# Softmax reciprocals turned through DRAM in a decoder layer's attention

## The chip, the cores and the metric

The kernel runs on one core of a Trainium2 chip. The core has five engines with a queue of instructions each: TensorE (PE in the profile, with its weight loads as PEld), VectorE (DVE), ScalarE (ACT), GpSimd (POOL) and SyncE (SP), which here only issues transfers. Engines wait for each other through semaphores. Transfers are issued by SP, ACT or POOL and are carried out by 16 DMA engines that all the issuers share. The metric is the device time of one execution in microseconds (us); lower is better.

## The reference

One decoder layer on x of 8 x 256 x 512, all in float32: self-attention with 16 heads of width 32, then an elementwise recurrence with the context (its decay is per head), then a feed-forward part (FFN) whose weights are splines of given control points. After each comes a residual and a layer norm. What matters here is the attention:

```python
q_r = jnp.einsum('bhtd,dr->bhtr', q, Wdown)
k_r = jnp.einsum('bhtd,dr->bhtr', k, Wdown)
v_r = jnp.einsum('bhtd,dr->bhtr', v, Wdown)
scores = jnp.einsum('bhqr,bhkr->bhqk', q_r, k_r) * scale
attn = jax.nn.softmax(scores, axis=-1)
y_r = jnp.einsum('bhqk,bhkr->bhqr', attn, v_r)
y = jnp.einsum('bhtr,rd->bhtd', y_r, Wup)
y = y.transpose(0, 2, 1, 3).reshape(B, T, D)
out = y @ Wo.T
```

The down and up projections are folded into the weights of q, k, v and of the output.

## The kernel before

The 2048 tokens (8 sequences of T = 256) are worked through in NG = 4 groups of 512 tokens, two sequences each. The projections of a group (`project`, 48 units of one matmul call in 12 chains) and the output projections of a finished sequence (`output`, units of the kind "o") are kept in the list `units`; `fill(n)` (321) takes n of them, and so puts them between the parts of the attention. The order of work is written by hand: the wrapper `Ordered` (266) keeps every engine's instructions in program order, so each engine's queue runs in the order in which the code below emits it.

The attention runs in 32 steps, `for s, (g, bb, quad) in enumerate(steps)` (701). A step is one quad of four heads of one sequence, n = 2g + bb; each sequence has quads 0 to 3. The steps are pipelined by one: in step s the scores (`scores`, 468) of step s + 1 are started, the exps of step s + 1 are emitted head by head with `ahead(0)` to `ahead(3)` (729), and the exps that step s - 1 has left in `es` are transposed (`transposed`, 502), copied out of PSUM (`evicted`, 509) by DVE, ACT, DVE and ACT in turn, and multiplied with v (`weighted`, 514).

- `exponentials` (486): DVE takes the negated maximum over the keys, `nmax`, with queries on the 128 partitions; ACT makes `e = exp(sc + nmax)` for each half of the queries and accumulates the sums, so that `sums[n]` is [128 queries, 2 halves, 16 heads].
- The four heads' score tiles `sc` lie in the four PSUM buffers of `ps_big`. The scores of the next step can only be written when the exps have read them.
- `weighted` writes `av`, a PSUM tile [128, 2, 256] whose partitions are (head of the quad, r) and whose free axis is the query; two quads share one `av`. It is not yet divided by the softmax sums.
- The division needs the reciprocal of the sums in the layout of `av`: the head on partitions, each value over 32 partitions, the query along the free axis. The sums lie the other way round. In odd quads (733 to 737) DVE takes the reciprocals `rec` of the eight heads of two quads and copies them 32 times, into `wide`. Late in the same step (756 to 767), behind `fill(6)`, PE turns `wide` round in four transposes into the PSUM tile `tr_rec`, and ACT copies that to `y` (tile yT in the profile).
- The pair `y, av` is left in `pending` (772). The next step multiplies it on DVE, `y = av * y` (745), behind the first eviction of that step; `output` then reads `y`. The last pair is multiplied behind the loop (775), just ahead of the FFN.

The pool `ps_mm` has four PSUM buffers, which transposes, projections, outputs, `tr_rec` and `av` share. In groups 0 to 2 `fill` finds the projections of the next group; in group 3 there are none, and each step takes `fill(2)` twice: outputs, and the first `inputs` (642) of the FFN, which turn x2 round, write it to DRAM and load it back in another order (`xd`, `md`, `xg`). Taps for the FFN weights are loaded by SP and combined by POOL all through the attention (`taps`, 387). ACT issues no transfers before the change but the seven at the very start (582 to 585).

The lines that decide where things stand in a step:

```python
        eTs.append(evicted(tr1, nc.scalar.copy))
        ahead(1)
        eTs.append(evicted(tr2, nc.vector.tensor_copy))
        fill(2)
        tr3 = transposed(es[3])
        ahead(2)
        eTs.append(evicted(tr3, nc.scalar.copy))
        ahead(3)
        fill(6 if g + 1 < NG else 2)
```

Of the kernel before, what the change touches and what calls it, by code (L numbers as in the profile page):

```python
# [10 lines left out]
F32 = mybir.dt.float32  # L11
# [6 lines left out]
P = 128  # L18
B, T, D = 8, 256, 512
NH, DH = 16, 32  # L20
# [262 lines left out]
def decoder_kernel(ctx: ExitStack, tc: tile.TileContext, x, xT, ctxT, wq, wkT, wvT, woT, wdownT, wup, decay, up_taps, down_taps, mom_f, sum_f, out, plan):  # L283
    nc = tc.nc
# [4 lines left out]
    small = ctx.enter_context(tc.tile_pool(name="small", bufs=4, side="left"))  # L289
    rows = ctx.enter_context(tc.tile_pool(name="rows", bufs=6, side="left"))  # L290
    ps_big = ctx.enter_context(tc.tile_pool(name="ps_big", bufs=4, space=PSUM))
    ps_mm = ctx.enter_context(tc.tile_pool(name="ps_mm", bufs=4, space=PSUM))
    ident = const.tile([P, P], F32, name="ident")
# [11 lines left out]
    done = ExitStack()  # L305
    last = done.enter_context(tc.tile_pool(name="last", bufs=1, side="right"))
    mid = ExitStack()
    att = mid.enter_context(tc.tile_pool(name="att", bufs=1, side="right"))
# [3 lines left out]
    nc = Ordered(tc)  # L312
# [8 lines left out]
    def fill(n):  # L321

        for i in range(n):
            if units:
                next(units[0][1])
                units[0][2] -= 1
                if not units[0][2]:
                    units.pop(0)
            if i % 2:
                slot()  # L330
                some_taps()
# [53 lines left out]
    folded, qkvs, rs, sums, xs, yTs = {}, {}, {}, {}, {}, {}  # L385
# [34 lines left out]
    def load_x(g):  # L420
        xT_g = early.tile([P, DC, GT], F32, tag="xT", name="xT_g")
        nc.sync.dma_start(out=xT_g, in_=xT[:, g * GT : (g + 1) * GT].rearrange("(c p) t -> p c t", p=P))
        return xT_g
# [24 lines left out]
    def projections(g, xT_g):  # L448
        qkvs[g] = group_tiles(g)
        return [[name, project(g, name, m, xT_g), DC] for name in "qkv" for m in range(DC)]  # L450

    def recur(n):

        r = last.tile([P, DC, T], F32, tag="r", name="r", bufs=2)
        nc.sync.dma_start(out=r, in_=ctxT[:, n * T : (n + 1) * T].rearrange("(c p) t -> p c t", p=P))
        rs[n] = r
        yield
        yield
        nc.gpsimd.tensor_tensor(r, r, r, ALU.mult)
        yield  # L460
        yield
        for ch in range(DC):
            nc.vector.tensor_tensor_scan(
                r[:, ch, :], dec[:, ch : ch + 1].to_broadcast([P, T]), r[:, ch, :], 0.0, ALU.mult, ALU.add
            )
            yield

    def scores(s):

        g, bb, quad = steps[s]  # L470
        qT, kT, _ = qkvs[g]
        t0 = bb * T
        sc = [ps_big.tile([P, 2, T], F32, tag="big", name="sc") for _ in range(4)]
        for qc in range(2):
            for j in range(4):
                at = slice(j * DH, (j + 1) * DH)
                nc.tensor.matmul(
                    sc[j][:, qc, :],
                    lhsT=qT[at, quad, t0 + qc * P : t0 + (qc + 1) * P],
                    rhs=kT[at, quad, t0 : t0 + T],  # L480
                    start=True,
                    stop=True,
                )
        return sc
# [17 lines left out]
    def transposed(e):  # L502
        tr = ps_mm.tile([P, 2, T], F32, tag="mm", name="tr_e")
        for kc in range(2):
            for qc in range(2):
                nc.tensor.transpose(tr[:, kc, qc * P : (qc + 1) * P], e[:, qc, kc * P : (kc + 1) * P], ident)
        return tr

    def evicted(tr, copy):
        eT = att.tile([P, 2, T], F32, tag="eT", name="eT", bufs=4)  # L510
        copy(eT, tr)
        return eT
# [16 lines left out]
    def load_rows(n):  # L529
        xs[n] = []  # L530
        for qc in range(2):
            x_t = rows.tile([P, D], F32, tag="row", name="x_t")
            r0 = (n * 2 + qc) * P
            nc.sync.dma_start(out=x_t, in_=x[r0 : r0 + P, :])
            xs[n].append(x_t)

    def output(n, qc):

        ps = ps_mm.tile([P, D], F32, tag="mm", name="ps_o")
        for c in range(DC):  # L540
            nc.tensor.matmul(
                ps,
                lhsT=yTs[n][c // 2][:, c % 2, qc * P : (qc + 1) * P],
                rhs=w_o[:, c, :],
                start=(c == 0),
                stop=(c == DC - 1),
            )
            if c < DC - 1:
                yield
        h1 = rows.tile([P, D], F32, tag="row", name="h1")  # L550
        s1 = small.tile([P, 1], F32, tag="s1", name="s1")
        nc.vector.scalar_tensor_tensor(h1, ps, 1.0, xs[n][qc], ALU.mult, ALU.add, accum_out=s1)
        chains.append(norms(n, qc, h1, s1))
        yield
# [78 lines left out]
    def open_inputs():  # L633
        pool = ctx.enter_context(tc.tile_pool(name="inputs", bufs=1, side="left"))
        ffn["pool"] = pool
        ffn["dram"] = ctx.enter_context(tc.tile_pool(name="dram", bufs=2, space=bass.MemoryType.DRAM))
        ffn["mf"] = pool.tile([P, DC, 2, K2], F32, name="mf")
        nc.sync.dma_start(out=ffn["mf"], in_=mom_f)
# [58 lines left out]

    pending = None  # L700
    for s, (g, bb, quad) in enumerate(steps):
        n = g * 2 + bb
        if quad == 0 and bb == 0:
            if g + 1 < NG:
                units += projections(g + 1, xT_g)
            else:
                first.close()
                open_inputs()
                units += [["i", inputs(0), 2 * DC], ["i", inputs(1), 2 * DC]]
        if quad == 0 and n:  # L710
            load_rows(n - 1)
            o = [["o", output(n - 1, qc), DC] for qc in range(2)]
            if bb and g + 1 < NG:
                units[1:1] = o[:1]
                units.append(o[1])
            else:
                units[1:1] = o
            chains.append(recur(n))
        more = s + 1 < len(steps)
        if more and steps[s + 1][0] != g:  # L720
            while any(u[0] != "o" for u in units):
                fill(4)
            if g + 2 < NG:
                xT_g = load_x(g + 2)
        if more:
            sc = scores(s + 1)
        after = []

        def ahead(j):
            if more:  # L730
                after.append(exponentials(s + 1, j, sc[j]))

        if quad % 2:
            rec = small.tile([P, 2, 8], F32, tag="rec", name="rec")
            nc.vector.reciprocal(rec, sums[n][:, :, quad // 2 * 8 : quad // 2 * 8 + 8])
            wide = att.tile([P, 2, 8, DH], F32, tag="wide", name="wide")
            nc.vector.tensor_copy(wide, rec.unsqueeze(3).to_broadcast([P, 2, 8, DH]))
        tr0 = transposed(es[0])
        ahead(0)
        eTs = [evicted(tr0, nc.vector.tensor_copy)]  # L740
        tr1 = transposed(es[1])
        tr2 = transposed(es[2])
        if pending is not None:
            y, av = pending
            nc.vector.tensor_tensor(y, av, y, ALU.mult)
            pending = None
# [4 lines that stand above are left out]
        tr3 = transposed(es[3])  # L751
        ahead(2)
        eTs.append(evicted(tr3, nc.scalar.copy))
        ahead(3)
        fill(6 if g + 1 < NG else 2)
        if quad % 2:
            tr = ps_mm.tile([P, 2, T], F32, tag="mm", name="tr_rec")
            for q in range(2):
                for qc in range(2):
                    nc.tensor.transpose(  # L760
                        tr[:, q, qc * P : (qc + 1) * P],
                        wide[:, qc, q * 4 : q * 4 + 4, :].rearrange("p h r -> p (h r)"),
                        ident,
                    )
            y = last.tile([P, 2, T], F32, tag="yT", name="yT", bufs=4)
            nc.scalar.copy(y, tr)
            yTs.setdefault(n, []).append(y)
        else:
            av = ps_mm.tile([P, 2, T], F32, tag="mm", name="av")
        weighted(s, eTs, av)  # L770
        if quad % 2:
            pending = y, av
        es = after
    y, av = pending
    nc.vector.tensor_tensor(y, av, y, ALU.mult)
# [204 lines left out]
```

## Time and profile before

| | |
|---|---|
| median of 3 runs | 632.89 us (632.06 to 634.3) |
| the profiled execution | 633.12 us |
| its span in the profile | 631.3 us, 9965 instructions |
| granted clock of TensorE | 0.996 |
| busy: PE, DVE, ACT, POOL | 604.9, 334.5, 277.6, 210.1 us |
| SP's queue (q1) | 35656 packets, 63.24 MB, 32.9% of 16 engines |
| ACT's queue (q10) | 1008 packets, 1.18 MB, 0.6% |
| POOL's queue (q0) | 2048 packets, 6.77 MB, 3.5% |
| packets under 512 B, all queues | 4776 |

In the profile every operation of the kernel carries the line of the wrapper, L275, so groups are told apart by the names of their tiles, written out<-in. A row of the timeline has the start in us from the span's start, the duration, the engine, the operation, how many were merged, and in brackets the idle time ahead of it with what ended it. A matmul call on float32 shows as two MATMUL records, a transpose as one; matmuls are pipelined, so four records of 274 ns each that follow each other take less than four times that. The engine name with a q (SPq, ACTq) is a sequencer issuing a transfer.

### The profile page before, as it was taken

Reading aid. Unit: us, or ns where it says so; the run is one execution under the profiler, and the core shown is the slowest. Engines: PE = TensorE matmul, PEld = TensorE weight load, DVE = VectorE, ACT = ScalarE, POOL = GpSimd, SP = SyncE. Lnnn points to the kernel's source line nnn. Section 1 sums busy time; section 2 is a strip of 40 time slices with the busy share of each in tenths; the row PEclk is TensorE's granted clock in tenths of the full one; section 3 lists DMA queues with packets and bytes.
Section 4 is the critical chain, followed back from the end, with each engine's and each line's share of the span. In section 5 each row is a group of like instructions: output and inputs, shape, how many; then the busy total and the mean of one; then the engine's idle time right before and its main releaser. Section 6 shows DMA issues by size and latency. Waiting matters only on the chain.

```text
span 631.3 us, 9965 instructions
## 1 busy us (share of the span) xinstructions
PE 604.9 (96%) x3436; PEld 306.5 (49%) x3436; DVE 334.5 (53%) x741; ACT 277.6 (44%) x820; POOL 210.1 (33%) x479
## 2 busy tenths in 40 slices
PE   6999999998999999999999999999999999999993
PEld 2544555554555545555545564444443444444542
DVE  0203545666884756974847787767073235307304
ACT  0114635547474556563556675652061134206202
POOL 0001986265624343733403122014303601520242
PEclk9999999999999999999999999999999999999998
DMA  8104252044214134314104646652047717744501
GB/s 303 39 0 149 82 183 85 20 134 151 54 47 152 51 96 138 84 47 137 34 2 151 152 106 172 182 175 68 2 141 221 204 40 228 195 125 142 176 18 67
DMA packets 38763, 71.83 MB, mean 114 GB/s; under 512 B 4776, under 2 KB 9128, under 8 KB 38584
## 3 DMA queue, kind: packets, MB, share of 16 engines
q1 hardware_dynamic: 35656, 63.24, 32.9%
q0 software_dynamic: 2048, 6.77, 3.5%
q10 hardware_dynamic: 1008, 1.18, 0.6%
q8 instruction: 27, 0.44, 0.3%
q14 instruction: 24, 0.20, 0.1%
HBM read 43.39 MB, written 11.01 MB: 86 GB/s over the span
## 4 chain that ended last, share of the span: by engine, by line
PE 85%; DVE 9%; ACT 3%; issue 1%; DMA 1%; POOL 0%; POOLq 0%; DVEq 0%; ACTq 0%
PE y L275 12%; PE ps_k L275 9%; PE ps_v L275 9%; PE ps_s L275 9%; PE ps_o L275 8%; PE ps_q L275 7%; PE tr_e L275 6%; PE sc L275 5%; PE pg L275 4%; PE av L275 4%; PE pu L275 4%; DVE nmax L275 3%; PE ps_mom L275 2%; ACT e L275 2%; DVE eT L275 2%
## 5 line engine op out<-in xcount | busy, mean ns | idle before, releaser
L275 ACT ACTIVATE e<-sc,nmax 128x256 f32<-128x256 f32 x256 | 120.0, 479 | 101.3 <-DVE nmax L275 101.2
L275 DVE TENSOR_REDUCE nmax<-sc 128x2 f32<-128x512 f32 x128 | 84.4, 681 | 73.0 <-PE sc L275 67.0
L275 POOL TENSOR_TENSOR taps<-taps 128x256 f32<-128x256 f32 (+1 forms) x144 | 89.1, 619 | 33.9 <-DMA taps<-in_down_taps 24.7
L275 PEld LDWEIGHTS tr_e<-ident,e 128*128 128x128 f32 x512 | 56.9, 140 | 25.3 <-issue 22.5
L275 PE MATMUL tr_e<-ident,e 128*128 128x128 f32 x512 | 68.3, 276 | 0.6 <-DVE eT L275 0.5
L275 PE MATMUL ps_k<-xT_g,w_k 128*128 128x512 f32 x128 | 61.6, 625 | 6.2 <-DMA xT_g<-in_xT 5.6
L275 PE MATMUL y<-inter,wd 32*128 32x512 f32 x512 | 64.0, 610 | 0.0
L275 PE MATMUL ps_o<-w_o,yT 128*128 128x512 f32 x128 | 60.0, 600 | 2.0 <-DVE eT L275 1.7
L275 PE MATMUL ps_v<-w_v,xT_g 128*128 128x512 f32 x128 | 58.6, 598 | 0.0
L275 PE MATMUL ps_q<-xT_g,w_q 128*128 128x512 f32 x128 | 58.2, 596 | 0.0
L275 PE MATMUL ps_s<-nat,sf 128*128 128x512 f32 x128 | 56.0, 595 | 0.0
L275 POOL TENSOR_SCALAR va<-ss 128x1 f32<-128x1 f32 x32 | 7.1, 220 | 144.3 <-ACT x L275 83.4
L275 ACT ACTIVATION_READ_ACCUMULATOR e<-sc,nmax 128x1 f32 x256 | 53.1, 208 | 0.0
L275 POOL TENSOR_TENSOR rs<-va,neghalf 128x1 f32<-128x1 f32 x48 | 28.1, 585 | 70.7 <-DVE va L275 68.0
L275 DVE TENSOR_TENSOR inter<-pu,sg 128x512 f32<-128x512 f32 x64 | 41.2, 686 | 14.8 <-ACT sg L275 11.3
L275 ACT ACTIVATE sg<-pg 128x512 f32<-128x512 f32 x64 | 37.4, 597 | 15.3 <-PE pg L275 15.0
L275 DVE COPY eT<-tr_e 128x512 f32<-128x512 f32 x64 | 43.7, 683 | 0.5 <-PE tr_e L275 0.4
L275 PE MATMUL av<-eT,v_g 128*32 128x256 f32 x512 | 36.7, 385 | 5.0 <-ACT eT L275 2.7
L275 PEld LDWEIGHTS ps_k<-xT_g,w_k 128*128 128x128 f32 x128 | 24.0, 199 | 32.1 <-issue 24.1
L275 PEld LDWEIGHTS y<-inter,wd 32*128 32x128 f32 x512 | 25.6, 184 | 28.7 <-issue 26.5
L275 PEld LDWEIGHTS ps_s<-nat,sf 128*128 128x128 f32 x128 | 24.0, 190 | 31.7 <-issue 29.2
L275 ACT COPY eT<-tr_e 128x512 f32<-128x512 f32 x64 | 37.4, 585 | 2.4 <-PE tr_e L275 2.4
(94 smaller groups left out, 741.6 us busy)
## 6 DMA issues: line engine op xcount, KB each, us to landing
nat<-inter SPq DMA_DIRECT2D x128, 128.0 KB
taps<-in_down_taps SPq DMA_DIRECT2D x40, 256.0 KB
taps<-in_up_taps SPq DMA_DIRECT2D x16, 384.0 KB
r<-in_ctxT SPq DMA_DIRECT2D x8, 512.0 KB
x_t<-in_x SPq DMA_DIRECT2D x16, 256.0 KB
out<-o SPq DMA_DIRECT2D x16, 256.0 KB
xT_g<-in_xT SPq DMA_DIRECT2D x3, 1024.0 KB
xg<-xd SPq DMA_DIRECT2D x4, 704.0 KB
```

The costliest lines, as they stand in the source:

```text
L275: return lambda *a, **k: self.tc.keep_in_program_order(f(*a, **k))
```

## The change

The copy to `wide`, the four transposes and ACT's copy to `y` go. In their place the reciprocals are written with the heads ahead of the halves, stored to a DRAM tile `rd` of [16, 128] by a transfer that ACT issues at the head of the step (each partition holds 16 values, and each goes to another row of `rd`, 512 bytes apart), and read back by two transfers, also issued by ACT, behind its second eviction. Each read takes the four heads of one quad, 1 KB of 256 queries each, and repeats each row over 32 partitions (`[0, DH]`). The reads wait for the store. `y` is taken from its pool at that place, and so ahead of `ahead(3)` and `fill`. `rd` has two buffers.

```diff
+    turned = done.enter_context(tc.tile_pool(name="turned", bufs=2, space=bass.MemoryType.DRAM))
     pending = None
     for s, (g, bb, quad) in enumerate(steps):
...
         if quad % 2:
-            rec = small.tile([P, 2, 8], F32, tag="rec", name="rec")
-            nc.vector.reciprocal(rec, sums[n][:, :, quad // 2 * 8 : quad // 2 * 8 + 8])
-            wide = att.tile([P, 2, 8, DH], F32, tag="wide", name="wide")
-            nc.vector.tensor_copy(wide, rec.unsqueeze(3).to_broadcast([P, 2, 8, DH]))
+
+            rec = small.tile([P, 8, 2], F32, tag="rec", name="rec")
+            at = slice(quad // 2 * 8, quad // 2 * 8 + 8)
+            nc.vector.reciprocal(rec, sums[n][:, :, at].rearrange("p q h -> p h q"))
+            rd = turned.tile([8 * 2, P], F32, tag="rd", name="rd")
+            nc.scalar.dma_start(out=rd.rearrange("k p -> p k"), in_=rec.rearrange("p h q -> p (h q)"))
         tr0 = transposed(es[0])
         ahead(0)
...
         tr3 = transposed(es[3])
         ahead(2)
         eTs.append(evicted(tr3, nc.scalar.copy))
+        if quad % 2:
+            y = last.tile([P, 2, T], F32, tag="yT", name="yT", bufs=4)
+            for q in range(2):
+                from_ = bass.AP(rd.tensor, rd.offset + q * 4 * T, [[T, 4], [0, DH], [1, T]])
+                nc.scalar.dma_start(out=y[:, q, :], in_=from_)
+            yTs.setdefault(n, []).append(y)
         ahead(3)
         fill(6 if g + 1 < NG else 2)
-        if quad % 2:
-            tr = ps_mm.tile([P, 2, T], F32, tag="mm", name="tr_rec")
-            for q in range(2):
-                for qc in range(2):
-                    nc.tensor.transpose(
-                        tr[:, q, qc * P : (qc + 1) * P],
-                        wide[:, qc, q * 4 : q * 4 + 4, :].rearrange("p h r -> p (h r)"),
-                        ident,
-                    )
-            y = last.tile([P, 2, T], F32, tag="yT", name="yT", bufs=4)
-            nc.scalar.copy(y, tr)
-            yTs.setdefault(n, []).append(y)
-        else:
+        if quad % 2 == 0:
             av = ps_mm.tile([P, 2, T], F32, tag="mm", name="av")
         weighted(s, eTs, av)
         if quad % 2:
-            pending = y, av
+            pending = yTs[n][-1], av
```

## The prediction

> **What bounds it now.** First the page's chain of work that ended last, by engine; then the windows view, cut where the attention's fill work runs out (335) and where it ends (404). The columns are the stretch, its sum, busy time and count of PE, PEld, DVE, ACT and POOL, the clock, the DMA share and GB/s.
>
> ```profile
> PE 85%; DVE 9%; ACT 3%; issue 1%; DMA 1%; POOL 0%; POOLq 0%; DVEq 0%; ACTq 0%
> ```
>
> ```profile
> 60.00:139.00 79.00, 78.78 (x461) 42.28 (x458) 43.38 (x83) 42.59 (x145) 52.22 (x96) 1.00 0.36 112
> 150.00:335.00 185.00, 182.70 (x1078) 98.31 (x1077) 124.04 (x282) 102.23 (x341) 77.76 (x142) 1.00 0.27 81
> 335.00:404.00 69.00, 62.78 (x474) 35.68 (x472) 54.08 (x128) 45.06 (x151) 15.13 (x23) 1.00 0.55 147
> ```
>
> Up to 335 TensorE is the path (busy 78.78 of 79.00, 182.70 of 185.00): each step (score, exp, transpose, weigh: about 11 us) is filled with projections of the next group, and DVE and ACT wait. The last group, 335 to 404, has little to fill with: PE drops to 62.78 of 69.00, DVE rises to 54.08, and transfers keep the DMA engines 0.55 busy. The chain in order of time for this stretch runs through DVE:
>
> ```profile
> 353.00 0.59 DVE eT L275
> 353.60 0.60 DVE yT L275
> 354.20 0.60 DVE nmax L275
> 354.80 0.60 DVE eT L275
> ```
>
> The second of these pieces is the multiply of av by y that the change will feed from a DMA.
>
> **What goes.** The change touches the 16 odd steps of 32 (quad 1 and 3), numbered 0 to 31 here. The groups view (busy, mean ns of one, idle before):
>
> ```profile
> L275 PE MATMUL tr_rec<-ident,wide 128*128 128x128 f32 x64 | 9.7, 274 | 0.8 <-DVE mom L275 0.8
> L275 ACT COPY yT<-tr_rec 128x512 f32<-128x512 f32 x16 | 9.4, 588 | 12.0 <-PE tr_rec L275 12.0
> L275 DVE COPY wide<-rec 128x512 f32<-128x512 f32 x16 | 9.3, 584 | 0.5
> ```
>
> PE: four transposes a step; from the first tr_rec to the first av is 0.53 us in the timeline (81.09 to 81.62), and PE's queue closes up by that. The ACT copy (0.59) and the DVE copy (0.43 at its median) lie in those engines' waits, except step 17, where a wide of 1.68 us stands on the chain at 251.98; its nmax then waits for PE's scores (begun at 251.79, 0.5 to the first pair), so about 1.2 us come back. Ten odd steps are clear of what follows (1 to 21 without 7): 10 x 0.53 + 1.2 = **6.5 us gained**. The permuted reciprocal has the same 16 elements (0.24 us) and costs nothing new.
>
> **What comes: the write.** ACT issues 128 x 16 single floats to DRAM, after the reciprocal. ACT idles there: in step 3 the reciprocal ends at 93.64, and the next exp starts at 95.57.
>
> ```profile
> 93.40 0.24 DVE L275 RECIPROCAL rec<-sums 128x16 f32<-128x16 f32 x1
> ...
> 95.57 0.47 ACT L275 ACTIVATE e<-sc,nmax 128x256 f32<-128x256 f32 x1 [5.60 <-DVE nmax L275]
> ...
> 98.89 0.58 ACT L275 COPY eT<-tr_e 128x512 f32<-128x512 f32 x1
> ```
>
> An issue from ACT takes 0.44 us (the decay load), so the issue is hidden. The landing matters because the two reads of y, which ACT issues behind its second eT copy (end 99.47), wait for it, with the exps of the fourth head and the next evictions queued behind them. Room from reciprocal to eT end: 5.83 us here, 5.53 to 10.31 in the other steps with a successor, 4.75 in the last. No row shows 4-byte stores. Fixed part: POOL's 256 KB xd store lands in 3.3 us; at the page's rate for SP's queue (63.24 MB in 32.9% of 16 engines over 631.3 us, 19.0 GB/s an engine) 0.9 of it is transfer, so 2.4. Per element, 128 to an engine: the queue rows give 93 ns for 1774 B (q1) and 60 ns for 1171 B (q10), a line through about zero, so the lower end is 2.4 us; the upper end lets each float cost a whole q10 packet, 128 x 60 ns, so 10.1. The rule that speaks against this is in the Trainium skill, "VectorE: DVE Perf Modes", section "The three transpose paths": a plain strided copy is 19 times slower than the crossbar's 1309 ns for 128x128 bf16, that is 24.9 us for 16384 elements; by proportion 3.1 us for 2048 (estimate), landing in 5.5. By the rows' line the write is free; by the rule it fits with the issue (5.94) just about into the room. I take 5.5: the line of the rows was drawn from packets of over a kilobyte. The excess in steps 9, 11 and 19 is 0.4 us; the fourth head's exps end 4.2 to 4.6 us ahead of the scores that reuse their PSUM, which covers it. In step 31 the reads go 1.2 late.
>
> **What comes: the reads.** y was ready when ACT's copy ended; now it must land before DVE's multiply in the next step, or DVE stops with nmax and eT queued behind, and ACT and PE wait for those. SP's 384 KB taps load gives the fixed part: issued at 94.56, its reader starts at 97.38; less 1.3 us at 304 GB/s is 1.5.
>
> ```profile
> 94.56 0.33 SPq L275 DMA_DIRECT2D taps<-in_up_taps  x1
> ```
>
> ```profile
> 97.38 0.73 POOL L275 TENSOR_TENSOR taps<-taps 128x256 f32<-128x256 f32 x1 [2.84 <-DMA taps<-in_up_taps]
> ```
>
> On 16 engines both reads (256 KB) take 0.9, and the second issue 0.4: y is there 2.8 us after eT's end. But the source's outer dimension counts 4 (heads). The Trainium skill, "DMA: Bandwidth & Descriptors", section "Why a DMA increments its semaphore by 16 and not by 1": a transfer runs on the largest k up to 16 that divides the outer dimension of both sides. Here k is 4: 256 KB at 4 x 19.0 GB/s is 3.45, y after 5.0 us. The trace bears the rule out: SP's 280 transfers carry 31,512 runs of data, and 35,656 packets less these is 4,144 completions, 336 short of 16 each, exactly what the rule takes off for the 44 whose outer dimension (1, 2, 3, 11, 20, 44) doesn't divide by 16. I take 5.0, plus 3.45 x the DMA share of the 5 us in question (between 0 and, packet for packet against 2 KB ones, twice that). Against the room, eT's end to the multiply, from the timeline:
>
> | step | eT end | multiply | room | share | y after | late |
> |---|---|---|---|---|---|---|
> | 7 | 146.06 | 149.48 | 3.4 | 0.50 | 6.7 | 3.3 |
> | 15 | 238.03 | 242.71 | 4.7 | 0.34 | 6.2 | 1.5 |
> | 23 | 330.97 | 335.65 | 4.7 | 0.28 | 6.0 | 1.3 |
> | 25 | 349.71 | 353.52 | 3.8 | 0.88 | 8.0 | 4.2 |
> | 27 | 366.09 | 370.15 | 4.1 | 0.38 | 6.3 | 2.2 |
> | 29 | 384.66 | 389.83 | 5.2 | 0.69 | 7.4 | 2.2 |
> | 31 | 401.56 | 404.56 | 3.0 | 0.65 | 7.2 | 4.2 |
>
> The other nine have 7.35 to 8.1 us of room and no lateness to speak of. Steps 8 and 16, which follow 7 and 15, are full of fill; DVE sits idle 3.17 us before 156.35, so I charge 0.5 and 0. Those after 23, 25, 27 and 29 lie in the last group, with DVE on the chain: 1.3 + 4.2 + 2.2 + 2.2 in full. The last multiply (4.2 + 1.2 late) holds up the first products of the FFN; its PSUM holds two pairs of projections, the third pu starts at 408.37, and would start at 404.56 + 5.4 + two DVE operations of 0.68, 411.3: 2.9. The two issues (0.9 us of ACT) also delay the fourth exps, where 7, 25 and 27 have only 0.1 to 0.7 us to spare; that lies beside the longer lateness. **Lost: 13.3 us.**
>
> **Sum.** The profiled execution took 633.12 (span 631.3 and 1.8 around it): 633.12 - 6.5 + 13.3 = 639.9; the median, 632.89, is 0.23 lower: **639.7**. About 0.3% (1.9 us) is what can be told from no change.
>
> **Rivals.** *The reads come in time* (26%): the instruction carries another outer dimension, or four engines do better than 19.0 GB/s. Then y is there after about 3 us; 13 steps keep 0.53, step 17 its 1.2, and the later exps in 7, 25 and 27 cost 1.5: 626.5. For it: nine steps have over 7 us of room. Against it: the count of completions. It decides when y lands within 3.8 us.
> *The write is slow* (14%): with 10.1 us each, ACT stands 4 to 5 us at the reads in most steps. The slack of 4.2 to 4.6 less the issues' 0.9 leaves some 1 us a step in eight, 8 us; y comes 15.5 us after the reciprocal, plus contention, which in 7, 15 and 23 to 31 adds 33; with nearly all gains gone, 673. It takes over from a landing of 5.6 us. For it: the skill's factor; against it: the rows' line.
> *Hidden both ways* (14%): half the lateness is taken up in waits and the sum is nought, 631 to 634.8.
>
> **How the numbers follow.** Forecast case 46% (634.8 to 648), slow write 14% above it: slower 0.60; same 0.14; faster 0.26. The range of 627 to 656 leaves a tenth on each side: the best of the timely reads, and the slowest writes.
>
> **What would show it.** Right: in the profile after, tr_rec, wide and the yT copy are gone; PE steps before 335 are 0.5 us shorter; DVE waits before yT multiplies for the DMA of y, 1 to 4 us each, in steps after 23, 25, 27, 29, 31; ACT's own waits for rd are under 1 us. Wrong: no such DVE waits (first rival), ACT waiting several us for rd in every odd step (second), or ACT's issues much longer than 0.44 us, which I have not priced.

## The result and the profile after

The changed kernel takes **758.17 us** (755.14 to 759.48) against 632.84 before: 1.1981 times as long, interval 1.1961 to 1.2. The direction was forecast, the size was not: 639.7 in a range of 627 to 656. The profiled execution took 759.48, its span is 757.7, TensorE's mean clock 0.916 instead of 0.996.

The page of the changed kernel: the packets, ACT's queue, and the chain by engine and by group.

```profile
DMA packets 76011, 76.16 MB, mean 101 GB/s; under 512 B 37928, under 2 KB 46376, under 8 KB 75832
...
q10 hardware_dynamic: 38256, 5.51, 4.6%
...
PE 49%; DMA 33%; DVE 6%; ACT 4%; POOL 4%; issue 3%; ACTq 2%; SPq 0%; POOLq 0%; DVEq 0%
DMA rd<-rec 20%; PE y L275 10%; PE ps_s L275 7%; DMA yT<-rd 7%; PE ps_k L275 4%; PE pg L275 4%; PE ps_v L275 4%; PE pu L275 4%; PE ps_q L275 3%; PE tr_e L275 3%; PE ps_o L275 3%; ACT e L275 3%; PE sc L275 2%; POOL taps L275 2%; DMA taps<-in_up_taps 2%
```

DMA was 1% of the chain and is 33%, and 20% of the chain is one group: the store of the reciprocals. ACT's queue went from 1008 packets to 38256. The difference is 16 stores of 2048 packets, one for each float (32768), 32 reads of 128 rows (4096), and 16 completions a store and 4 a read (384). The last term bears out the four engines of a read.

The chain of the changed kernel in order of time, over the steps that the prediction counted as filled (start, us, what):

```profile
109.18 0.25 DVE rec L275
109.45 11.48 DMA rd<-rec
...
122.09 1.03 ACT e L275 x4
...
123.17 1.13 PE sc L275 x10
124.29 2.04 PE tr_e L275 x12
126.33 2.82 PE ps_v L275 x4
...
135.86 11.67 DMA rd<-rec
...
148.18 5.01 DMA yT<-rd
...
153.29 0.69 DVE yT L275
```

The end is set by a loop that has no arithmetic of size in it: reciprocal, store (11.5 us), two issues of reads, the exps queued behind them, the scores that those exps make room for. Once more (135.86) the chain goes on through the reads to the multiply by y. PE comes in last and slow: twelve transposes take 2.04 us and four records of a projection 2.82. The same stretch in the chain of the first kernel:

```profile
106.29 1.46 PE tr_e L275 x12
107.75 1.94 PE ps_v L275 x4
```

ACT's timeline in the first of these steps (brackets: idle before, releaser):

```profile
114.67 0.58 ACT L275 COPY eT<-tr_e 128x512 f32<-128x512 f32 x1
120.95 1.09 ACTq L275 DMA_DIRECT2D yT<-rd  x2
122.09 0.47 ACT L275 ACTIVATE e<-sc,nmax 128x256 f32<-128x256 f32 x1 [6.85 <-issue]
```

From the end of the eviction, 115.25, ACT stands at the reads for 5.70 us. The bracket puts all 6.85 us down to "issue", which is true of 1.09 only; the rest is the wait of the first read for the store. This is how a wait at an issuing instruction looks here, and why the waits view carries it under two names:

```profile
ACT e L275 <- issue: 55.6, 8, 7.9
ACT e L275 <- DMA yT<-rd: 51.4, 6, 19.1
DVE yT L275 <- DMA yT<-rd: 42.7, 11, 17.6
...
POOL taps L275 <- DMA taps<-in_down_taps: 73.5, 16, 10.4
```

(us, times, longest.) The first two rows are ACT behind the reads, 107 us with the issues themselves. The third is the wait forecast at DVE, far larger. The last has nothing to do with the division: POOL waits for SP's loads of taps 73.5 us, where it waited 24.7 before.

The windows view of the changed kernel; the stretches end at the scores of step 4, at those of step 24, with which the last group begins, and at the end of the attention:

```profile
60.00:110.00 50.00, 35.17 (x186) 19.16 (x188) 16.30 (x27) 16.96 (x58) 33.86 (x63) 0.83 0.45 102
110.00:397.00 287.00, 245.72 (x1310) 132.32 (x1306) 148.18 (x332) 122.20 (x416) 98.35 (x187) 0.91 0.37 75
397.00:510.00 113.00, 84.81 (x532) 49.67 (x524) 57.55 (x131) 49.36 (x167) 15.83 (x25) 0.83 0.52 93
```

The first kernel goes from 60 to the same places in 34, 231 and 79 us, with a clock (the third column from the end) of 1.00 in each:

```profile
60.00:94.00 34.00, 33.78 (x197) 18.09 (x198) 17.37 (x30) 18.59 (x63) 29.42 (x54) 1.00 0.47 146
94.00:325.00 231.00, 226.63 (x1348) 122.44 (x1340) 154.53 (x343) 126.45 (x425) 105.96 (x196) 1.00 0.28 85
325.00:404.00 79.00, 72.78 (x555) 41.88 (x554) 59.17 (x137) 51.75 (x173) 15.88 (x25) 1.00 0.49 130
```

To place the loss, take the time from the start of one step's scores to that of the next, in both traces. **Interval k** runs from the scores of step k to those of k + 1, mostly while iteration k - 1 of the loop is at work; a read that iteration k issues late shows in interval k + 2. The expectations below say "step" for these intervals. Most even ones, the odd iterations without their four transposes, are 0.44 us shorter.

| interval | after less before, us |
|---|---|
| 3 (read of iteration 1) | +17.6 |
| 5 to 25, the eleven odd ones and 10 | +68.4 |
| 27, 29, 31 | +15.7, +6.2, +5.7 |
| first product of the FFN to its first down product | +20.2 |
| all others | -7.5 |
| whole execution | +126.3 |

In the FFN stretch both new transfers stand one behind the other on the chain of the changed kernel, with nothing left to lie under them, and TensorE starts cold:

```profile
503.88 11.91 DMA rd<-rec
...
516.44 12.36 DMA yT<-rd
...
533.45 0.85 PE pg L275 x2
...
537.52 0.43 PE pg L275 x2
```

### The profile page after: what moved, and what is told of

The parts are those of the page before. It is cut to its first block, busy times and chain, and to the rows that moved or that the text cites. A ratio compares the mean times of both kernels' runs of the same rounds, so it can differ in the third digit from the quotient of the medians.

```text
span 757.7 us, 9928 instructions
## 1 busy us (share of the span) xinstructions
PE 640.9 (85%) x3372; PEld 326.7 (43%) x3372; DVE 327.1 (43%) x725; ACT 270.8 (36%) x804; POOL 206.6 (27%) x479
## 3 DMA queue, kind: packets, MB, share of 16 engines
q0 software_dynamic: 2048, 6.77, 4.9%
## 4 chain that ended last, share of the span: by engine, by line
PE 49%; DMA 33%; DVE 6%; ACT 4%; POOL 4%; issue 3%; ACTq 2%; SPq 0%; POOLq 0%; DVEq 0%
DMA rd<-rec 20%; PE y L275 10%; PE ps_s L275 7%; DMA yT<-rd 7%; PE ps_k L275 4%; PE pg L275 4%; PE ps_v L275 4%; PE pu L275 4%; PE ps_q L275 3%; PE tr_e L275 3%; PE ps_o L275 3%; ACT e L275 3%; PE sc L275 2%; POOL taps L275 2%; DMA taps<-in_up_taps 2%
## 5 line engine op out<-in xcount | busy, mean ns | idle before, releaser
L275 PE MATMUL sc<-k_g,q_g 32*128 32x256 f32 x512 | 57.7, 469 | 69.1 <-ACT e L275 69.1
L275 POOL TENSOR_TENSOR taps<-taps 128x256 f32<-128x256 f32 (+1 forms) x144 | 86.9, 603 | 93.0 <-DMA taps<-in_down_taps 73.5
L275 PE MATMUL tr_e<-ident,e 128*128 128x128 f32 x512 | 82.6, 315 | 0.7 <-DVE eT L275 0.5
L275 PEld LDWEIGHTS tr_e<-ident,e 128*128 128x128 f32 x512 | 69.5, 163 | 29.7 <-issue 23.7
L275 PEld LDWEIGHTS sc<-k_g,q_g 32*128 32x128 f32 x512 | 32.6, 211 | 92.9 <-ACT e L275 75.6
L275 PE MATMUL ps_o<-w_o,yT 128*128 128x512 f32 x128 | 62.3, 619 | 2.6 <-DVE eT L275 2.6
L275 PE MATMUL pg<-xg,wg 64*128 64x512 f32 x128 | 41.2, 617 | 16.7 <-DVE yT L275 16.7
L275 DVE TENSOR_TENSOR inter<-pu,sg 128x512 f32<-128x512 f32 x64 | 41.9, 688 | 15.6 <-ACT sg L275 10.5
L275 PE MATMUL av<-eT,v_g 128*32 128x256 f32 x512 | 38.9, 391 | 11.1 <-ACT eT L275 6.0
L275 ACT COPY eT<-tr_e 128x512 f32<-128x512 f32 x64 | 37.4, 585 | 12.8 <-PE tr_e L275 12.7
```

What stands on the lines that cost most here:

```text
L275: return lambda *a, **k: self.tc.keep_in_program_order(f(*a, **k))
```

## The experiments

How long a store takes to land is read from the trace's completion events, from the start of the issue to the 16th. Each "landing" below is the median over the stores of the run, with the extremes (16 stores; 15 in e10, 11 in e8, and 14 in e2, where the events of two are incomplete).

| kernel | us | ratio to before | landing of the store, us |
|---|---|---|---|
| after: 2048 pieces of 4 B | 758.17 | 1.1981 [1.1961, 1.2] | 12.06 (10.76 to 14.77) |
| e3_double: 4096 of 4 B | 872.58 | 1.3796 [1.3732, 1.386] | 18.48 (16.16 to 20.1) |
| e4_pairs: 1024 of 8 B | 666.53 | 1.0538 [1.0517, 1.0559] | 5.28 (4.54 to 8.58) |
| e1_rows64: 128 of 64 B | 658.34 | 1.0413 [1.0396, 1.0431] | 1.43 (1.39 to 3.36) |
| e5_pe_rows: 16 of 512 B | 662.2 | 1.0474 [1.0459, 1.049] | 1.39 (1.33 to 5.02) |
| e6_pe_rows_k16: the same, reads on 16 engines | 658.27 | 1.0401 [1.0374, 1.0428] | 1.51 (1.34 to 4.35) |
| e7_reads_sp: as after, reads issued by SP | 732.99 | 1.1593 [1.1564, 1.1623] | 11.59 (10.43 to 14.05) |
| e2_unwaited: before, and the store, unread | 660.51 | 1.0457 [1.0387, 1.0527] | 13.16 (12.52 to 18.83) |
| e9_unwaited_rows: before, and the 64 B store, unread | 632.19 | 1.0002 [0.9993, 1.001] | 1.68 (1.39 to 4.67) |
| e10_from3: e8 with the last group by DRAM too | 651.22 | 1.03 [1.0282, 1.0319] | 1.39 (1.33 to 4.3) |
| e8_hybrid: by DRAM in odd steps 3 to 23 only | 628.64 | 0.9944 [0.9928, 0.9959] | 1.39 (1.33 to 4.35) |

**e1_rows64: the same bytes in rows.**

```diff
-            rd = turned.tile([8 * 2, P], F32, tag="rd", name="rd")
-            nc.scalar.dma_start(out=rd.rearrange("k p -> p k"), in_=rec.rearrange("p h q -> p (h q)"))
+            rd = turned.tile([P, 8 * 2], F32, tag="rd", name="rd")
+            nc.scalar.dma_start(out=rd, in_=rec.rearrange("p h q -> p (h q)"))
```

> The store writes the same 8 KB, but as 128 runs of 64 bytes, one to a partition, in place of 2048 single floats; the two dependent reads are as in the changed kernel. It leaves out the turning round, so y holds the reciprocals in another order. Theory A (the store's landing grows with the number of its single elements, and ACT stands at the reads for it): the store lands 2.5 to 3.5 us after its issue, ACT waits under 1 us for it, and the time is that of the forecast made with a short store, 630 to 645. Rival B (a store to DRAM with a dependent read on the same queue costs this whatever its pieces are): the landing stays at 11 to 12 us and the time at about 758. Rival C (the late y at DVE's multiply, from reads on four engines, is the greater part): ACT's waits go, the time stays above 690.

658.34 us: about 100 of the 126 us hang on the pieces of the store, and the expected time was still missed by 13 us. By interval, the even ones keep their gains (-0.44, -0.8 and -1.04), nothing is lost between 5 and 24, and three intervals lose 10.9 (3), 10.3 (27) and 10.3 (31), with 2.1 at the FFN. Interval 3, in the chain of e1_rows64:

```profile
83.77 3.33 DMA taps<-in_up_taps
87.17 1.12 ACTq L275
88.31 0.53 ACTq L275
88.89 1.03 ACT e L275 x4
```

ACT's read leaves at 87.17, though its store had landed at 72.8. It leaves when a load of taps lands that SP issued, and that load had waited for POOL. The semaphore events say why: the transfers issued by SP and ACT signal their completion on eight semaphores (100 to 107) in turn, and each of the 335 in this trace leaves only after the one before it on its semaphore has landed. The read of iteration 1 follows that load on 107, where the load's last completion stands at 87.09. The kernel's text names no such dependence.

In the last group it is the reads. First SP's timeline of e1_rows64, then its chain:

```profile
351.24 4.11 SPq L275 DMA_DIRECT2D xg<-xd  x6
```

```profile
335.51 4.78 DMA yT<-rd
...
353.68 13.57 DMA yT<-rd
...
398.94 14.39 DMA yT<-rd
```

In iteration 23 the read lands 4.8 us after its second issue. In iterations 25 and 29 SP issues loads of `xg` just ahead of it and around it; the first packet of y moves 6.2 us after the issue (iteration 25), and y lands after 13.6 and 14.4.

**e2_unwaited: the store alone.** The kernel before, with the store added and nobody reading it:

```diff
+            rd = turned.tile([8 * 2, P], F32, tag="rd", name="rd")
+            nc.scalar.dma_start(out=rd.rearrange("k p -> p k"), in_=rec.rearrange("p q h -> p (q h)"))
```

> The kernel before, with the store of 2048 single floats from ACT added at its place; nothing reads it, y comes from the transposes. Theory A: the store costs only its issue (0.36 us of ACT in a wait), 632 to 637. Rival D (the store itself holds up the DMA engines, so that other transfers come late and the kernel with them): POOL's waits for taps rise from 28 to over 60 us as in the changed kernel, and the time is above 650.

660.51 us, and so 28 us for a transfer that no instruction reads. POOL, at 0% of the chain before, is at 7%, and its waits for the loads of taps rise as in the changed kernel. The waits view of the kernel before, then that of e2_unwaited:

```profile
POOL taps L275 <- DMA taps<-in_down_taps: 24.7, 12, 6.6
```

```profile
POOL taps L275 <- DMA taps<-in_down_taps: 74.3, 16, 11.4
```

These loads are late because they are slow on the way: in e2 one of 256 KB takes 8.84 us from issue to landing (median of 23) where a store is in flight during that time, and 2.66 us (median of 17) where none is. The pages show it in SP's queue, which moves the same packets and bytes in both kernels. Before, they occupied the engines for 32.9% of 631.3 us, in e2 for 39.0% of 656.4, 256 us in place of 208:

```profile
q1 hardware_dynamic: 35656, 63.24, 32.9%
```

```profile
q1 hardware_dynamic: 35656, 63.24, 39.0%
```

From 103.3 to 112.0, between the last packet record of a store and its landing, the DMA engines of e2 are 67% busy and move 29 GB/s. Over all such stretches SP's packets of 3072 bytes take 1.11 us on average, elsewhere 0.15. So rival D holds: the store slows other transfers, and the kernel with them. SP itself does not stand behind the store's completion: none of its transfers leaves within 1.2 us of the landing of the store that had its semaphore before.

A wait at a shared semaphore shows at one store of ACT's. In the chain of e2_unwaited it leaves when a load of SP's on the same semaphore has landed:

```profile
95.75 3.34 DMA x_t<-in_x
...
99.17 0.38 ACTq L275
```

**e3_double and e4_pairs: what the landing depends on.** Twice as many floats, of which the reads take the first half (a second reciprocal of 0.25 us fills the other); and half as many pieces of twice the size:

```diff
-            rec = small.tile([P, 8, 2], F32, tag="rec", name="rec")
+            rec = small.tile([P, 2, 8, 2], F32, tag="rec", name="rec")
...
-            nc.scalar.dma_start(out=rd.rearrange("k p -> p k"), in_=rec.rearrange("p h q -> p (h q)"))
+            nc.scalar.dma_start(out=rd.rearrange("k p -> p k"), in_=rec.rearrange("p i h q -> p (i h q)"))
```

> The changed kernel with the reciprocals stored twice in one transfer, 4096 single floats, of which the reads take the first half. Theory A: the landing goes from 11.5 us to about 20.5 (2.5 fixed, 4.5 ns an element), ACT stands 9 us longer in each of the 16 odd steps, time 758 + 140 = about 900. Rival B: landing and time as in the changed kernel, 758 to 770.

```diff
-            nc.scalar.dma_start(out=rd.rearrange("k p -> p k"), in_=rec.rearrange("p h q -> p (h q)"))
+            rd = turned.tile([8, P, 2], F32, tag="rd", name="rd")
+            nc.scalar.dma_start(out=rd.rearrange("k p c -> p k c"), in_=rec)
```

> The changed kernel with the store in 1024 runs of 8 bytes in place of 2048 of 4 (the bytes are the same; the two halves of the queries lie next to each other, so y holds the reciprocals in another order). Theory A: landing about 7 us (2.5 fixed and 1024 x 4.5 ns), ACT's wait mostly gone, 650 to 685. If the price were by bytes or fixed (rival B): 11 to 12 us and about 758.

872.58 and 666.53 us. The chain of e3_double has the store at its new length in the first of its stalls:

```profile
113.42 19.03 DMA rd<-rec
```

Over the five kinds of store the landing follows the pieces, not the bytes: at equal bytes 12.06, 5.28, 1.43 and 1.39 us for 2048, 1024, 128 and 16 pieces. It isn't a straight line: from 1024 to 2048 pieces each engine's 64 more cost 106 ns apiece, from 2048 to 4096 its 128 more cost 50.

**e5_pe_rows and e6_pe_rows_k16: few pieces in the right order, and the reads' engines.** e5 turns `rec` round first, by one transpose to [16, 128] and a copy by ACT; e6 then reads each head alone, so that the outer dimension counts 32 and the read runs on 16 engines:

```diff
+            tr = ps_mm.tile([8 * 2, P], F32, tag="mm", name="tr_rec")
+            nc.tensor.transpose(tr, rec.rearrange("p h q -> p (h q)"), ident)
+            recT = att.tile([8 * 2, P], F32, tag="recT", name="recT", bufs=2)
+            nc.scalar.copy(recT, tr)
...
+            nc.scalar.dma_start(out=rd, in_=recT)
```

```diff
-            for q in range(2):
-                from_ = bass.AP(rd.tensor, rd.offset + q * 4 * T, [[T, 4], [0, DH], [1, T]])
-                nc.scalar.dma_start(out=y[:, q, :], in_=from_)
+            for j in range(4):
+                from_ = bass.AP(rd.tensor, rd.offset + j * T, [[0, DH], [4 * T, 2], [1, T]])
+                nc.scalar.dma_start(out=y[j * DH : (j + 1) * DH], in_=from_)
```

> The changed kernel with the 16 reciprocals of a query turned by one small transpose on TensorE and a copy of 16 x 128 on ACT, and stored as 16 rows of 512 bytes; the reads are as in the changed kernel. Theory A (the single floats of the store are what was mis-sized): the store lands within 3 us and the time is within 1% of the run with 64-byte pieces, 650 to 664, and of the 125 us over before some 100 are gone. The rest should stand in the same three places: about 11 us in step 3, where ACT waits for a taps load of SP that shares a completion semaphore with the read, and about 10 us each in steps 27 and 31, behind reads that share the engines with the xg loads. Rival B: about 758.

> As the run with the small transpose, but y is read by four transfers of one head each (outer dimension 32) in place of two of one quad each (outer dimension 4). Theory E (four engines make the reads late in the last group): the reads land in about 3 us where nothing else runs, against 5, DVE's waits for y in the last group fall below 5 us in all, and the time is 10 to 20 us under that of the two reads. Rival F (the reads are late because they queue behind the 1.3 MB of xg loads that SP issues just ahead, on however many engines): the waits in the last group stay at 8 us or more each, and the time within 6 us of the other, two more issues on ACT included.

662.2 and 658.27 us. The late reads of iterations 25 and 29 land 13.05 and 13.47 us after the second issue in e5. In the chain of e6_pe_rows_k16 stand the first of the four reads of iteration 25 and the last of iteration 29:

```profile
359.70 8.05 DMA yT<-rd
...
404.01 9.41 DMA yT<-rd
```

There y is complete 9.63 and 9.41 us after the last issue. Sixteen engines take 3.4 to 4.1 us off the 13; the rest stays, where a read with no `xg` ahead of it lands in 4.2 to 5.5 us on four engines (e5) and in 2.0 to 2.1 in most steps on sixteen (e6). So the place behind the loads costs more than the four engines do. DVE's waits for y fall from 21.4 us (e5) to 12.3: 6.5 in the waits view, and 5.8 in iteration 25 that the view puts down to `xg`, though the last read lands 0.19 us ahead of the multiply. The total falls by 4 only: interval 3 costs 10.5 in e6 (8.2 in e5), and 27 and 31 still 7.4 and 6.5. Interval 2 loses some 4.4 in both: there ACT's store waits for a load of taps on its semaphore, and in e5 leaves at 75.01, 3.7 us after the copy ahead of it has ended.

**e7_reads_sp: the wait moved from ACT to SP.**

```diff
-                nc.scalar.dma_start(out=y[:, q, :], in_=from_)
+                nc.sync.dma_start(out=y[:, q, :], in_=from_)
```

> The changed kernel with the two reads issued by SP in place of ACT, at the same place of the program; the store stays with ACT. If ACT's standing at the reads is what costs (A), the slack of DVE's multiply hides part: y lands about 12 + 6 us after the reciprocal against 13 to 14 of room, 4 to 5 us late a step, of which some 3 are hidden in the filled steps; with the last group in full, 670 to 700. If the lateness of y alone sets the time (C), it stays at 745 to 765. SP's own waits behind the store would make it slower than that.

732.99 us, between the two values. ACT no longer stands at the reads and interval 3 loses nothing, but 100 of the 125 us stay. The waits view of e7_reads_sp:

```profile
DVE yT L275 <- DMA yT<-rd: 103.8, 15, 20.1
POOL taps L275 <- DMA taps<-in_down_taps: 100.3, 20, 13.0
```

DVE's wait for y, 42.7 us before this edit, is now 103.8: who waits is another engine, while the store lands as late as before (11.59 us).

**e9_unwaited_rows: the issue without the slow landing.** As e2, with 64-byte rows:

```diff
-            nc.scalar.dma_start(out=rd.rearrange("k p -> p k"), in_=rec.rearrange("p q h -> p (q h)"))
+            nc.scalar.dma_start(out=rd, in_=rec.rearrange("p q h -> p (q h)"))
```

> The kernel before, with a store from ACT that nothing reads, as in the earlier run of that kind, but in 128 runs of 64 bytes in place of 2048 floats. If that run lost its 28 us because the store is slow to land and SP's transfers, which take the same eight completion semaphores in turn, wait for it (G), this one is at 632 to 640. If it lost them because any transfer of ACT has to wait its turn behind SP's (H), it is within 6 us of it, 652 to 662.

632.19 us, ratio 1.0002 [0.9993, 1.001]. Sixteen more issues on ACT cost nothing, so the 28 us of e2 belong to the slow landing, not to ACT's issuing. The time is the one expected of G, but for another reason: beside these short stores a 256 KB load of taps lands in 2.63 us, as without them (2.64), where e2 has 8.84.

**e8_hybrid and e10_from3: DRAM only where there is room.** e8 takes e5's way in the odd steps 3 to 23, and the old one in step 1 (whose read meets the load of taps) and in the last group; e10 takes the old way in step 1 alone.

```diff
+        by_dma = quad % 2 and s > 1 and g + 1 < NG
+        if by_dma:
...
+            rd = turned.tile([8 * 2, P], F32, tag="rd", name="rd")
+            nc.scalar.dma_start(out=rd, in_=recT)
+        elif quad % 2:
```

```diff
-        by_dma = quad % 2 and s > 1 and g + 1 < NG
+        by_dma = quad % 2 and s > 1
```

> The turn through DRAM (small transpose, rows of 512 bytes, two reads) only in the odd steps 3 to 23; step 1 and the last group take wide, transposes and copy as before. If the loss of the run with the small transpose in all steps stands in exactly two places, the read of step 1 (tied to a taps load by its semaphore) and the reads of the last group (behind the xg loads), both are gone, and what is left is the gain it showed between steps 4 and 25, 3.7 us: 628 to 630, faster than before by 0.4 to 0.7%. If the reads disturb elsewhere once these are gone, it is at 632 or above.

> As the other kernel of this pair, but with the last group turned through DRAM too; only step 1 keeps the old way. If the two places are independent, the last group costs here what it cost before (about 21 us) and step 1 nothing: 632.2 - 3.7 + 21 = 648 to 652. If the tie by shared semaphores only moves to another transfer when step 1 is taken out, a step between 3 and 9 is long by 5 us or more, and the time 655 to 662.

628.64 us for e8, 0.9944 [0.9928, 0.9959]: faster than both kernels of the case, than the first by 0.6%. Its page has a chain like the first kernel's, with more PE in it:

```profile
PE 89%; DVE 5%; ACT 2%; DMA 2%; issue 1%; POOL 0%; ACTq 0%; POOLq 0%; DVEq 0%
```

e10 is at 651.22. Its only difference is the last group, where its chain has the reads behind `xg` again (13.45 and 13.97 us in iterations 25 and 29): intervals 27 and 31 lose 10.1 and 9.2, the FFN 2.2. The way through DRAM costs 22.6 us there, with a store that lands early.

## Why the prediction was wrong, and where it was right

**The step that failed is the write.** "I take 5.5: the line of the rows was drawn from packets of over a kilobyte." It lands 12.06 us after the start of its issue (11.70 after its end, as the forecast counted), beyond the upper end of 10.1 as well. The lower end priced bytes; the proportion that was taken comes to 1.5 ns a float (24.9 us for 16384), the upper end to 60 ns a float on its engine. Measured, 1920 more pieces for the same bytes (e1 to the changed kernel) cost 10.6 us, 5.5 ns each, or 89 on its engine. So the term was mis-sized, and ACT, which was to wait under 1 us for `rd`, stands at the reads. What the store does to the other transfers was put at nothing, without a reason. That it makes one piece for each float stands in the Trainium skill, "DMA: Bandwidth & Descriptors", section "Rules for kernel authors" (a last dimension that isn't contiguous becomes one descriptor per element); the packets of the page after agree to the last one. A piece more cost 50 to 106 ns on its engine; the upper end's 60 lay between.

**The rival had the mechanism, with its slope too flat.** "ACT stands 4 to 5 us at the reads in most steps" became 5.70 in the step shown. But the slack that "leaves some 1 us a step in eight" became 2.5 to 11.6 in the intervals 5 to 25. Four terms were missing:

- *The late y in filled steps.* It was charged to steps 7, 15 and 23 to 31 only. In e7, with ACT free of the reads, DVE waits for y 103.8 us, 29.8 of them in eight steps that were charged with nothing, with nmax and eT queued behind it: the fill does not cover that.
- *Transfers beside the store are slow.* A slow store alone costs 28 us (e2), a fast one nothing (e9), since the loads beside it take 8.84 us and not 2.66. In the changed kernel it is 8.05 with a store in flight and 2.79 without.
- *Whoever shares a completion semaphore waits too.* In interval 3 a fast store's read stands behind a load that POOL held up: 10.9 us in e1, none in e10, which spares that step. The trace of the first kernel shows such a wait at its start, where ACT issues transfers: SP's load of `w_v` leaves at 9.08, when ACT's load of `xT_g` on the same semaphore has landed (9.06).
- *TensorE's clock.* After such a stall twelve transposes take 2.04 us, not 1.46, and four records of a projection 2.82, not 1.94: 1.5 us for a stall. The granted clock there is 0.50 from 125.01 to 128.42, and in the changed kernel it stands at 0.50 in 15 stretches from 84 to 535 us, each 3.41 us or a multiple, 123 us in all. At the FFN two products take 0.85, and 0.43 some 4 us later. PE's busy time rose from 604.9 to 640.9, though the 9.7 of `tr_rec` are gone. The Trainium skill, "TensorE: Matmul & The Clock Gate", Part 1, says that an idle window of about 3.4 us halves the clock and that as long a busy one restores it. The half and the length agree: 3.4 us at half speed lose 1.7 us a stall (estimate by the page), the rows show 1.5. The idle time does not: ahead of this stretch PE stood still for 1.97 us only (121.19 to 123.17). The prediction priced stalls by their length only.

**The reads' contention was too small.** "3.45 x the DMA share" gave y 8.0 us after eT in step 25 and 7.4 in step 29; behind the second issue alone the read took 13.6 and 14.4 in e1. The share is a mean over the engines; what delays y, by the order of the transfers, is what SP has queued just ahead. Of the 13.3 us forecast as lost, 12.8 lay in the last group and at the FFN; e10 lost 22.6 there.

**What held.** The gain: 0.53 us was forecast for each odd step, 0.44 came in most; over the ten steps counted (intervals 2 to 22 without 8) e1 gains 5.3 us against 6.5, of it 1.04 in step 17, where 1.2 + 0.53 was forecast. The four engines: reads take 5.01 us in the chain after the second issue, some 5.6 from the first, where 5.0 was forecast. The issue of the store: 0.36 to 0.40 us, forecast 0.44. The last product's delay once the store is fast: 2.1 us, forecast 2.9. With the write mended, step 1 spared and 22.6 in place of 12.8, the sum is 633.1 - 6.5 + 23.1 = 649.7, near e10's 651.22. As the 22.6 is itself e10 less e8, this bears out the rest of the sum alone, 627.1 against e8's 628.64. The direction was right in part by luck: the reads of the last group do make the kernel slower (e10), but some 100 us of the 126 come from the store, which was counted as fitting into the room.

**Open.** That the reads wait in the engines' queues behind `xg` is argued from the order and the 6.2 us to the first packet; moving the `xg` loads wasn't tried, nor was another assignment of semaphores. What the engines do between the last packet record of a store and its landing no view shows. How the changed kernel's loss divides between ACT at the reads, the slowed loads and the clock was not separated, and e2's and e7's shares of it can't be added.

## What to carry to other kernels

Price a store to DRAM by its contiguous pieces, not its bytes, and turn data round on the chip first when that makes the pieces long: one transpose and a copy bought a landing of 1.39 us for one of 12. Many small pieces also hold up the transfers of all other issuers while they land (e2). Before a transfer gets a new issuer, look at what the other issuers send just ahead of it and who shares its completion semaphores, for these order engines that have no data in common. A slow transfer is not hidden because its reader is far off; use the room step by step, as e8 does.

## What was not expected of the hardware

- The packet records of the store do not show its cost: in the step of the chain above, all 2064, those of the 16 completions included, lie within 1.5 us (110.48 to 111.93, 7 to 9 ns each for the floats), and the completions' events come 8.3 to 11.5 us after the issue.
- A store that nothing reads made this kernel 28 us slower (e2): while it landed, other packets of 3072 bytes took 1.11 us in place of 0.15.
- A read of 128 KB issued behind SP's loads of `xg` moved its first packet 6.2 us later, and landed after 13 to 14.4 us on four engines and 9.4 to 9.6 on sixteen.
- The granted clock of TensorE fell to 0.50 after it had stood still for 1.97 us.
